# A scan and mixture-of-experts kernel: the output begins as x + D times the normalized row instead of as a copy of x

## The chip, the core and the metric

The kernel runs as one program on one core of a Trainium2 chip. The metric is the device time of one execution in microseconds (us); smaller is better. A core has TensorE (PE, matrix products; PEld is its weight load), VectorE (DVE), ScalarE (ACT), GpSimd (POOL) and SyncE (SP). [...] DMA transfers are issued from the queues of SP and POOL.

## The reference, cut to what matters

A layer normalization feeds two branches, and both are added to the input. The attention branch sorts the tokens of each batch into clusters, runs a selective state-space scan over the sorted sequence, and puts the result back in the tokens' own order. The other branch is a mixture of eight experts with two chosen for each token. x is 2 x 2048 x 256 floats.

```python
xn = _layernorm(x)                      # (x - mean) / sqrt(var + 1e-5)
...
def step(h, inp):                       # over the sorted tokens u = sorted xn
    dA = exp(d_t[..., None] * A)
    h = dA * h + (d_t * u_t)[..., None] * b_t[:, None, :]
    y = einsum('bdn,bn->bd', h, c_t)
...
return y + D[None, :, None] * u         # the term that the change moves
...
x = x + scan_branch(xn) + expert_branch(xn)
```

D is one number per channel (256 of them). The term D * u, put back into the tokens' order, is D * xn of the same token, so it does not depend on the sorting.

## The kernel before

**The front** (lines 134 to 1018) works on all 4096 tokens, eight tiles `xts[k]` of 128 partitions x 4 rows x 256 channels (and 4 columns for expert numbers and shares). VectorE finds mean and variance (L374, `find_norm` L405), TensorE finds scores of clusters and experts, ScalarE normalizes seven of the tiles in place (L429, 128x256 at a time) and VectorE the eighth (L433); each tile is then stored to the DRAM tensor `xn` (L437). `route` lists which tokens belong to which expert tile. Its function `list_tokens` runs eight rounds; each builds two bf16 factors `one` and `num` on VectorE (L327, L330, L337) and ScalarE (L336) and multiplies them on TensorE (L342). In the front these factors are taken from the pool `tok`, the eight buffers that the `xts` held. `sort_tokens` and `list_rows` make the same sort of list for the clusters. `small_weights` (L274) makes small constants, among them `diag`, the 128x128 matrices with D on the diagonal, one for each half of the channels.

**The output** is gathered by addition in DRAM. Each of its rows begins as the row of x: `begin_sums(k)` (L990) is a DMA of 512 KB from x to out, DRAM to DRAM, four of them early in the front and four at its end. Later the expert tiles and the scan pieces add their rows with indirect DMAs that accumulate (`add_rows`, L884, on POOL's queue). The first of these waits until all eight beginnings have landed.

**The scan** is cut into 8 pieces of 512 sorted tokens (two batches, four pieces each). A piece's rows are gathered (`gather_scan`, L628), turned into `u` (channels x tokens: TensorE L653, ScalarE copy L654), projected (L667, L674), copied to `xd` (L679) and sent through DRAM to be broadcast. From this come the step sizes `dl` and `du`. For the first piece that is `size_first` (L759), one chain through TensorE, ScalarE and VectorE; for the others `size` and `series` are spread over the piece before. A piece has 8 steps (4 quarters of the 16 states, 2 halves of the channels), a step 4 places. At each place VectorE multiplies (L840) and scans (L849) 128x512 elements, ScalarE makes the decay (L834), and TensorE turns the states of the step before (L861) and, at the last place, contracts them with the C rows (L870) into the PSUM tile `y` of that half.

That `y` is begun by `Piece.begin(h)` (L792): four matmuls `u` x `diag` per half, which put D * u there; the contractions then add to it, and ScalarE takes the sums out (L805). In the trace one float matmul has two records, so a piece has 16 records of line L796.

**The expert tiles**, 71 of 128 rows, are dealt among the places. A tile is three jobs: `up(0)` and `up(1)` (L954, 16 records each, the first with a tanh on ScalarE at L962), then `down` (L977, scaled out by ScalarE at L981 and added to the output). VectorE's two products, `silu` (L967) and `gate` (L971), follow their `up` two places later. The up products have one PSUM buffer each (`ps_h`, `bufs=1`), so the next tile's `up(0)` waits for `silu`, and `up(1)` for `gate`. The tiles' weights come by indirect DMA (L914) into three buffers. A planner with written-down costs (`at_place`, 0.9 for each `begin`) keeps the planned work on TensorE in a fixed ratio to that on VectorE, and so decides at which place a job goes. `keep_order` fixes each engine's order to that of the text.

**The lead** (L1078) stands between front and scan: the first seven jobs of the expert tiles, with the preparation of the first piece between them.

```python
lead = [
    [], [p.find_members], [], [lambda: p.turn(0), lambda: p.turn(1)],
    [lambda: p.project(0), lambda: p.project(1), p.end_projection, ..., p.size_first, ...],
    [], [lambda: p.begin(0), lambda: p.begin(1)],
]
```

Job 0 and 1 are `up(0)` and `up(1)` of expert tile 0, jobs 2 and 3 those of tile 1, job 4 is `down` of tile 0, jobs 5 and 6 are the up products of tile 2.

Of the kernel before, what the change touches and what calls it, by code (L numbers as in the profile page):

```python
# [39 lines left out]
F32 = mybir.dt.float32  # L40
BF16 = mybir.dt.bfloat16
I32 = mybir.dt.int32
AF = mybir.ActivationFunctionType
# [5 lines left out]
P = 128  # L49
# [7 lines left out]
def scan_moe_kernel(  # L57
# [47 lines left out]
    ps_h = ctx.enter_context(tc.tile_pool(name="ps_h", bufs=1, space=PSUM))  # L105
    ps_m = ctx.enter_context(tc.tile_pool(name="ps_m", bufs=2, space=PSUM))
    front = ctx.enter_context(ExitStack())
    tok = front.enter_context(tc.tile_pool(name="tok", bufs=8))
    sml = front.enter_context(tc.tile_pool(name="sml", bufs=1))
# [125 lines left out]
    nc.sync.dma_start(bias, dt_bias)  # L235
    dcol = cst.tile([P, ND], F32, name="dcol")
    nc.sync.dma_start(dcol, ds_)
    na = cst.tile([P, ND, NS], F32, name="na")
# [35 lines left out]
    def small_weights():  # L274

        diag = cst.tile([P, ND, P], F32, name="diag")
        for h in range(ND):
            nc.vector.tensor_scalar(diag[:, h, :], ident, dcol[:, h : h + 1], None, ALU.mult)


        cp = cst.tile([K, XP], F32, name="cp")
        nc.vector.memset(cp, 0.0)
        differ = cst.tile([P, ND, K], F32, name="differ")
        nc.vector.tensor_copy(differ[:, :, 0:1], chosen_by[:, :, 0:1])
        nc.vector.tensor_sub(differ[:, :, 1:], chosen_by[:, :, 1:K], chosen_by[:, :, 0 : K - 1])
        pc = ps_m.tile([K, NS], F32, tag="m", name="pc")
        for h in range(ND):
            nc.tensor.matmul(
                pc, lhsT=differ[:, h, :], rhs=pwT[:, h, :], start=h == 0, stop=h == ND - 1
            )  # L290
        nc.vector.tensor_copy(cp[:, R + NS :], pc)

        nc.scalar.activation(na, na, AF.Exp)
        nc.vector.tensor_scalar_mul(na, na, -1.0)
        return diag, cp

# [57 lines left out]
    def front_factors(width: int):  # L354

        one = tok.tile([P, P, LC], BF16, tag="tok", name="one")
        num = tok.tile([P, 3, width, LC], BF16, tag="tok", name="num")
        return one, num
# [46 lines left out]
    def find_norm():  # L405


        nm = sml.tile([P, BJ], F32, tag="nm", name="nm")
        nc.vector.tensor_add(nm, st[:, :, 1], st[:, :, 4])
# [11 lines left out]
        nc.vector.tensor_mul(nr, nm, rstd)  # L421
        return nm, rstd, nr

# [214 lines left out]
    class Piece:  # L638
# [152 lines left out]

        def begin(self, h: int):  # L792

            y = ps_s.tile([P, JC, P], F32, tag=f"y{h}", name=f"y{h}")
            for i in range(JC):
                nc.tensor.matmul(  # L796
                    y[:, i, :], lhsT=self.u[:, h, i * P : (i + 1) * P], rhs=diag[:, h, :],
                    start=i == 0, stop=False, skip_group_check=True,
                )
            self.ys[h] = y  # L800

        def take_sums(self, h: int):
# [21 lines left out]
    class Step:  # L824
# [19 lines left out]
        def scan(self, i: int):  # L844
            p, q, h = self.piece, self.q, self.h
            if i == 0:
                self.hs = late.tile([P, CH, Q], F32, tag="hs", name="hs", bufs=3)
            start = carry[:, q, h, i : i + 1] if p.c else 0.0
# [18 lines left out]
        def contract(self, i: int):  # L867
            p, q = self.piece, self.q
            for j in range(P // G):
                nc.tensor.matmul(  # L870
                    p.ys[self.h][j * G : (j + 1) * G, i, :],
                    lhsT=p.zs[q][:, i * (P // G) + j, :], rhs=self.ht[i][:, j, :],
                    start=False, stop=q == NQ - 1, skip_group_check=True,
                )
# [112 lines left out]
    n_x = len(xts)  # L987
    acc_rows = [(out_rows[r : r + CH, :], x.rearrange("b l d -> (b l) d")[r : r + CH, :]) for r in range(0, B * L, CH)]

    def begin_sums(k: int):  # L990
        nc.sync.dma_start(*acc_rows[k])

    for k in range(n_x):
# [4 lines left out]
        if k == n_x // 2:  # L998
            turn_scores(0)
        if k < n_x // 2:  # L1000
            begin_sums(k)
    score((n_x - 2, n_x - 1))
    turn_scores(1)
    nm, rstd, nr = find_norm()
    for k in range(n_x - 1):
# [8 lines left out]
    pieces[0].gather()  # L1014
    diag, cp = small_weights()
    for k in range(n_x // 2, n_x):
        begin_sums(k)
    front.close()
# [49 lines left out]
    for t in range(n_dealt + 1):  # L1068
        if t < n_dealt:
            jobs += [part_up(t, 0), part_up(t, 1)]  # L1070
        if t > 0:
# [3 lines left out]
    p = pieces[0]  # L1075


    lead = [  # L1078
        [], [p.find_members], [], [lambda: p.turn(0), lambda: p.turn(1)],
        [lambda: p.project(0), lambda: p.project(1), p.end_projection, lambda: p.load_b(0, Q), p.size_first,  # L1080
         *(lambda q=q: p.load_z(q) for q in range(NQ))],
        [], [lambda: p.begin(0), lambda: p.begin(1)],
    ]
    ahead = len(lead)
    for n, more in enumerate(lead):
# [4 lines left out]
        for _, do in later.pop(now, []):  # L1090
            do()
    for i in range(Q):
        steps[0].decay(i)
# [23 lines left out]
    for n, p in enumerate(pieces):  # L1117
# [3 lines left out]
        if n:  # L1121
# [16 lines left out]
            at_place(s1 + 5, NSUB - 1, lambda p=p: p.load_b(0))  # L1138
            at_place(s0, 3, lambda p=p: p.begin(0), 0.9)
            at_place(s0 + 1, 1, lambda p=p: p.begin(1), 0.9)  # L1140
        s2 = s0 + SP_
# [140 lines left out]
```

## Time and profile before

| what | value |
|---|---|
| three runs, median | 751.91 us (751.2 to 751.93) |
| the profiled execution | 752.28 us |
| its span, as in the profile | 750.5 us (1.8 us lie around it) |
| mean clock granted to TensorE | 0.951 of full speed |
| busy PE / PEld / DVE / ACT / POOL | 678.0 / 588.9 / 678.5 / 508.0 / 523.0 us |
| records of L796 (D * u on TensorE) | 128, mean 292 ns, 18.5 us in sum |
| DMAs x to out | 8 of 512 KB, 8.3 us to landing |

The span runs from the first instruction to the last. "Busy" counts an engine's time inside instructions; TensorE's records overlap each other (the pitch from one to the next is far below the mean duration), so its busy time is not the time that it needs. The chain is the work that ended last, followed back from release to release. A line with "idle before" tells how long an engine stood before an instruction and which engine released it.

### The profile page before, as it was taken

What the parts mean: (1) busy time and instruction counts of PE and PEld (TensorE: products, weight loads), DVE (VectorE), ACT (ScalarE), POOL (GpSimd) and SP (SyncE); (2) the same over time, 40 slices, a digit from 0 to 9 for tenths busy, and PEclk for the clock granted to TensorE, in tenths of its full rate; (3) what the DMA queues carried; (4) which work ended last, traced back from release to release, by engine and by line L of the source; (5) the groups of instructions that cost most, each with busy time, mean ns of one, the idle gap of its engine ahead of it and who ended that gap; (6) DMA issues with size and microseconds to landing.
All of it is one profiled execution on the core that took longest, in us unless ns stands there. A gap on an engine that the chain in (4) does not pass through costs nothing.

```text
span 750.5 us, 16877 instructions
## 1 busy us (share of the span) xinstructions
PE 678.0 (90%) x6506; PEld 588.9 (78%) x6506; DVE 678.5 (90%) x1085; ACT 508.0 (68%) x983; POOL 523.0 (70%) x362
## 2 busy tenths in 40 slices
PE   7375779999998999999999999999999998999993
PEld 5144678888877998888878898999798977899982
DVE  8885389899987999999999999999999997999991
ACT  4830446686758866886769577967795768767762
POOL 2023448667777788777877887788788888887733
PEclk9755979999999999999999999999999999999996
DMA  8676544584436755685458656865575547745312
GB/s 269 243 162 233 166 162 92 159 244 138 124 56 171 252 146 117 171 264 148 114 132 281 160 130 124 255 198 132 119 249 157 128 93 219 227 125 118 86 17 29
DMA packets 60401, 120.31 MB, mean 160 GB/s; under 512 B 24160, under 2 KB 41248, under 8 KB 53152
## 3 DMA queue, kind: packets, MB, share of 16 engines
q0 software_dynamic: 38784, 63.71, 36.0%
q1 hardware_dynamic: 21536, 55.50, 21.9%
q8 instruction: 52, 0.85, 0.5%
q14 instruction: 29, 0.24, 0.1%
HBM read 170.78 MB, written 22.28 MB: 257 GB/s over the span
## 4 chain that ended last, share of the span: by engine, by line
PE 69%; ACT 11%; DVE 9%; DMA 5%; issue 4%; POOL 1%; POOLq 0%; ACTq 0%; DVEq 0%
PE p_ps L954 29%; PE py L977 13%; PE pt_s L861 11%; PE y L870 7%; DMA w<-in_w_down_dram,w_row 3%; ACT ht L865 3%; PE y L796 2%; PE pl L342 2%; PE pt_g L937 2%; DMA out_dram<-yo,token_of 2%; ACT da L834 2%; DVE st L374 1%; ACT e L732 1%; ACT r L732 1%; PE px L667 1%
## 5 line engine op out<-in xcount | busy, mean ns | idle before, releaser
L954 PE MATMUL p_ps<-xT,w 128*128 128x128 f32 x2176 | 272.6, 281 | 12.3 <-DVE g L971 8.1
L954 PEld LDWEIGHTS p_ps<-xT,w 128*128 128x128 f32 x2176 | 258.0, 195 | 26.3 <-DVE g L971 8.3
L849 DVE TENSOR_TENSOR_SCAN hs<-da,carry,bu 128x512 f32<-128x512 f32 x192 | 246.0, 1281 | 0.0
L834 ACT ACTIVATE da<-dl,na 128x512 f32<-128x512 f32 x256 | 183.7, 734 | 0.2 <-DVE dl L789 0.2
L840 DVE TENSOR_TENSOR bu<-du,bt 128x512 f32<-128x512 f32 x256 | 173.1, 676 | 0.0
L865 ACT COPY ht<-pt_s 128x512 f32<-128x512 f32 x256 | 138.4, 595 | 40.3 <-PE pt_s L861 39.3
L895 POOL DMA_INDIRECT out_dram<-yo,token_of x68 | 131.4, 1932 | 48.0 <-ACT yo L981 22.6
L914 POOL DMA_INDIRECT w<-in_w_up_dram,w_row x68 | 91.8, 1350 | 89.2 <-DVE w_row L595 43.4
L861 PE MATMUL pt_s<-ident,hs 128*128 128x128 f32 x1024 | 136.8, 277 | 9.7 <-ACT ht L865 8.6
L977 PE MATMUL py<-w,g 128*128 128x256 f32 x544 | 129.8, 381 | 7.5 <-ACT xT L939 4.8
L861 PEld LDWEIGHTS pt_s<-ident,hs 128*128 128x128 f32 x1024 | 116.5, 142 | 21.4 <-ACT ht L865 13.4
L977 PEld LDWEIGHTS py<-w,g 128*128 128x128 f32 x544 | 98.0, 190 | 20.6 <-ACT xT L939 6.0
L928 POOL DMA_INDIRECT xg_sb<-xn,token_of x68 | 91.8, 1349 | 26.2 <-issue 12.8
L914 POOL DMA_INDIRECT w<-in_w_down_dram,w_row x68 | 94.7, 1392 | 20.7 <-issue 13.4
L895 POOL DMA_INDIRECT out_dram<-yt,line_of x32 | 66.1, 2065 | 23.0 <-issue 11.3
L849 DVE TENSOR_TENSOR_SCAN hs<-da,bu 128x512 f32<-128x512 f32 x64 | 78.1, 1221 | 0.0
L962 ACT ACTIVATE t_sb<-p_ps 128x512 f32<-128x512 f32 x68 | 41.0, 603 | 54.5 <-PE p_ps L954 54.4
L870 PE MATMUL y<-ht,z 128*32 128x128 f32 x2048 | 74.0, 277 | 1.5 <-PEq L1208 0.7
L981 ACT ACTIVATE yo<-py,own 128x256 f32<-128x256 f32 x68 | 32.3, 475 | 61.4 <-PE py L977 58.8
L967 DVE SCALAR_TENSOR_TENSOR t_sb<-t_sb,p_ps 128x512 f32<-128x512 f32 x68 | 45.8, 674 | 26.1 <-ACT t_sb L962 26.1
L870 PEld LDWEIGHTS y<-ht,z 128*32 128x32 f32 x2048 | 50.8, 109 | 19.6 <-issue 10.2
L632 POOL DMA_INDIRECT xs<-xn,line_of x32 | 41.8, 1306 | 14.7 <-issue 8.2
(202 smaller groups left out, 582.0 us busy)
## 6 DMA issues: line engine op xcount, KB each, us to landing
bt<-bc SPq DMA_DIRECT2D x31, 1024.0 KB, 5.1
z<-bc SPq DMA_DIRECT2D x32, 256.0 KB, 3.2
xn<-xt SPq DMA_DIRECT2D x8, 520.0 KB, 2.6
xt<-in_x_dram SPq DMA_DIRECT2D x8, 512.0 KB, 8.0
out_dram<-in_x_dram SPq DMA_DIRECT2D x8, 512.0 KB, 8.3
w<-in_w_up_dram,w_row POOLq DMA_INDIRECT x68
w<-in_w_down_dram,w_row POOLq DMA_INDIRECT x68
xg_sb<-xn,token_of POOLq DMA_INDIRECT x68
```

The source lines that it names most:

```text
L834: nc.scalar.activation(self.da[i], self.piece.dl[:, self.h, :], AF.Exp, scale=na[:, self.h, n : n + 1])
L840: nc.vector.tensor_mul(self.bu[i], self.piece.du[:, self.h, :], self.piece.bts[self.q][:, i, :])
L849: nc.vector.tensor_tensor_scan(self.hs[:, :, i], self.da[i], self.bu[i], start, ALU.mult, ALU.add)
L861: nc.tensor.transpose(pt[:, j, :], self.hs[:, t0 : t0 + G, :].rearrange("p t n -> p (t n)"), ident)
L865: nc.scalar.copy(self.ht[i], pt)
L870: nc.tensor.matmul(p.ys[self.h][j * G : (j + 1) * G, i, :], lhsT=p.zs[q][:, i * (P // G) + j, :], rhs=self.ht[i][:, j, :], start=False, st ...
L895: ins = nc.gpsimd.indirect_dma_start(out=out_rows, out_offset=bass.IndirectOffsetOnAxis(ap=numbers, axis=0), in_=rows, in_offset=None, com ...
L914: nc.gpsimd.indirect_dma_start(out=to[self.t % NW], out_offset=None, in_=rows, in_offset=bass.IndirectOffsetOnAxis(ap=w_row[:, self.t : se ...
L928: nc.gpsimd.indirect_dma_start(out=self.xg, out_offset=None, in_=xn_d, in_offset=bass.IndirectOffsetOnAxis(ap=token_of[:, self.t : self.t ...
L954: nc.tensor.matmul(p[:, f, :], lhsT=wk[:, h, f * P : (f + 1) * P], rhs=self.xT[:, h, :], start=h == 0, stop=h == ND - 1,)
L967: nc.vector.scalar_tensor_tensor(self.s, self.s, 1.0, self.p1, ALU.add, ALU.mult)
L977: nc.tensor.matmul(py, lhsT=self.g[:, f, :], rhs=w2[:, f, :], start=f == 0, stop=f == NH - 1)
```

## The change

The eight `xts` tiles live longer: their pool `tok` is moved to the other end of the memory and stays open through the lead. After a tile was normalized, it is turned into the row that the output begins with, in place. With std = (var + eps) * rstd and the row r already normalized,

(D + std) * r + mean = D * r + x.

VectorE does the first step (`scalar_tensor_tensor`, add then mult, 128x256), ScalarE adds the mean (Identity with the mean as bias, 128x256), four rows for each tile, so 32 instructions on each engine, and SP stores the tile to the output (8 DMAs of 512 KB from SBUF). This is spread over the first four jobs of the lead. The copies of x, `diag` and the 64 `u` x `diag` matmuls go, with the planner's 0.9 for each `begin`; the first contraction of a piece starts its PSUM tile. The factors `one` and `num` of the front are now in six buffers of the scan's `da` and four of `pre`'s `tok`. The states `hs` of the scan have a pool of their own, opened where the `xts` were, so the first scan waits until the eight stores are done.

```diff
+    rows_of = ctx.enter_context(ExitStack())
+    tok = rows_of.enter_context(tc.tile_pool(name="tok", bufs=8, side="right"))
-    tok = front.enter_context(tc.tile_pool(name="tok", bufs=8))
...
-    dcol = cst.tile([P, ND], F32, name="dcol")
-    nc.sync.dma_start(dcol, ds_)
+    drow = cst.tile([P, D], F32, name="drow")
+    nc.sync.dma_start(drow, ds_.partition_broadcast(P))
...
-        diag = cst.tile([P, ND, P], F32, name="diag")
-        for h in range(ND):
-            nc.vector.tensor_scalar(diag[:, h, :], ident, dcol[:, h : h + 1], None, ALU.mult)
...
-        one = tok.tile([P, P, LC], BF16, tag="tok", name="one")
-        num = tok.tile([P, 3, width, LC], BF16, tag="tok", name="num")
+        one = scn.tile([P, P, LC], BF16, tag="da", name="one", bufs=6)
+        num = pre.tile([P, 3, width, LC], BF16, tag="tok", name="num")
...
-        def begin(self, h: int):
-            y = ps_s.tile([P, JC, P], F32, tag=f"y{h}", name=f"y{h}")
-            for i in range(JC):
-                nc.tensor.matmul(
-                    y[:, i, :], lhsT=self.u[:, h, i * P : (i + 1) * P], rhs=diag[:, h, :],
-                    start=i == 0, stop=False, skip_group_check=True,
-                )
-            self.ys[h] = y
...
-                self.hs = late.tile([P, CH, Q], F32, tag="hs", name="hs", bufs=3)
+                self.hs = states.tile([P, CH, Q], F32, tag="hs", name="hs")
...
+            if q == 0 and i == 0:
+                p.ys[self.h] = ps_s.tile([P, JC, P], F32, tag=f"y{self.h}", name=f"y{self.h}")
...
-                    start=False, stop=q == NQ - 1, skip_group_check=True,
+                    start=q == 0 and i == 0, stop=q == NQ - 1, skip_group_check=True,
...
+    def find_rest():
+        nc.vector.tensor_mul(std, ve, rstd)
+        nc.vector.tensor_scalar_mul(mean, nm, -1.0)
     def begin_sums(k: int):
-        nc.sync.dma_start(*acc_rows[k])
+        for i in range(JC):
+            j = k * JC + i
+            row = xts[k][:, i, 0:D]
+            nc.vector.scalar_tensor_tensor(row, drow, std[:, j : j + 1], row, ALU.add, ALU.mult)
+            nc.scalar.activation(row, row, AF.Identity, bias=mean[:, j : j + 1])
+        b, j0 = k * JC // J, k * JC % J
+        nc.sync.dma_start(
+            out[b].rearrange("(p j) d -> p j d", j=J)[:, j0 : j0 + JC, :], xts[k][:, :, 0:D]
+        )
...
-        if k < n_x // 2:
-            begin_sums(k)
...
-    for k in range(n_x // 2, n_x):
-        begin_sums(k)
+    find_rest()
...
     lead = [
-        [], [p.find_members], [], [lambda: p.turn(0), lambda: p.turn(1)],
+        [p.find_members, begin(0), begin(1)], [begin(2), begin(3)], [begin(4), begin(5)],
+        [begin(6), lambda: p.turn(0), lambda: p.turn(1), begin(7)],
...
-        [], [lambda: p.begin(0), lambda: p.begin(1)],
+        [], [],
     ]
...
+    rows_of.close()
+    states = ctx.enter_context(tc.tile_pool(name="states", bufs=3, side="right"))
...
-            at_place(s0, 3, lambda p=p: p.begin(0), 0.9)
-            at_place(s0 + 1, 1, lambda p=p: p.begin(1), 0.9)
```

In the changed kernel `begin(k)` in the lead stands for `begin_sums(k)`; its three parts are lines L992 (VectorE), L993 (ScalarE) and L995 (the store).

More of the change, by code (lines that the diff above doesn't have):

```diff
@@ L294, in small_weights @@
         nc.vector.tensor_scalar_mul(na, na, -1.0)
-        return diag, cp
+        return cp
     def over(v, last_dim):
@@ L405, in find_norm @@
     def find_norm():
-        nm = sml.tile([P, BJ], F32, tag="nm", name="nm")
+        nm = cst.tile([P, BJ], F32, name="nm")
         nc.vector.tensor_add(nm, st[:, :, 1], st[:, :, 4])
@@ L421, in find_norm @@
         nc.vector.tensor_mul(nr, nm, rstd)
-        return nm, rstd, nr
+        return nm, rstd, nr, ve
     def normalize(k: int, on_act: bool):
@@ L987, in scan_moe_kernel @@
     n_x = len(xts)
-    acc_rows = [(out_rows[r : r + CH, :], x.rearrange("b l d -> (b l) d")[r : r + CH, :]) for r in range(0, B * L, CH)]
-    def begin_sums(k: int):
-        nc.sync.dma_start(*acc_rows[k])
+    std = cst.tile([P, BJ], F32, name="std")
+    mean = cst.tile([P, BJ], F32, name="mean")
+    def find_rest():
+        nc.vector.tensor_mul(std, ve, rstd)
+        nc.vector.tensor_scalar_mul(mean, nm, -1.0)
+    def begin_sums(k: int):
+        for i in range(JC):
[7 more added lines that the diff above has]
+        )
     for k in range(n_x):
@@ L999, in scan_moe_kernel @@
             turn_scores(0)
-        if k < n_x // 2:
-            begin_sums(k)
     score((n_x - 2, n_x - 1))
     turn_scores(1)
-    nm, rstd, nr = find_norm()
+    nm, rstd, nr, ve = find_norm()
     for k in range(n_x - 1):
@@ L1014, in scan_moe_kernel @@
     pieces[0].gather()
-    diag, cp = small_weights()
-    for k in range(n_x // 2, n_x):
-        begin_sums(k)
+    cp = small_weights()
+    find_rest()
     front.close()
@@ L1075, in scan_moe_kernel, with begin @@
     p = pieces[0]
+    def begin(k: int):
+        return lambda: begin_sums(k)
     lead = [
-        [], [p.find_members], [], [lambda: p.turn(0), lambda: p.turn(1)],
+        [p.find_members, begin(0), begin(1)], [begin(2), begin(3)], [begin(4), begin(5)],
+        [begin(6), lambda: p.turn(0), lambda: p.turn(1), begin(7)],
         [lambda: p.project(0), lambda: p.project(1), p.end_projection, lambda: p.load_b(0, Q), p.size_first,
          *(lambda q=q: p.load_z(q) for q in range(NQ))],
-        [], [lambda: p.begin(0), lambda: p.begin(1)],
+        [], [],
     ]
@@ L1265 @@
         "a_logs": columns(L0_attn_A_logs),
-        "ds": columns(L0_attn_Ds),
+        "ds": np.asarray(L0_attn_Ds)[None],
         "w_up": np.concatenate([rows(L0_ffn_w1), rows(L0_ffn_w3)], axis=2),
```

## The prediction

> **What bounds the kernel now.** I read the page's shares and its chain first, then the waits of the scan stage (98 to 740 us), then the ScalarE and TensorE rows of the lead.
>
> ```profile
> PE 678.0 (90%) x6506; PEld 588.9 (78%) x6506; DVE 678.5 (90%) x1085; ACT 508.0 (68%) x983; POOL 523.0 (70%) x362
> ...
> PE 69%; ACT 11%; DVE 9%; DMA 5%; issue 4%; POOL 1%; POOLq 0%; ACTq 0%; DVEq 0%
> PE p_ps L954 29%; PE py L977 13%; PE pt_s L861 11%; PE y L870 7%; DMA w<-in_w_down_dram,w_row 3%; ACT ht L865 3%; PE y L796 2%; PE pl L342 2%; PE pt_g L937 2%; DMA out_dram<-yo,token_of 2%; ACT da L834 2%; DVE st L374 1%; ACT e L732 1%; ACT r L732 1%; PE px L667 1%
> ```
>
> TensorE and VectorE are equally busy, but the chain runs through TensorE, and L796 is 2% of it. The waits of the scan stage (us in total, times, longest) tell who waits for whom:
>
> ```profile
> DVE t_sb L967 <- ACT t_sb L962: 20.2, 12, 4.4
> ...
> PE pt_s L861 <- ACT ht L865: 8.6, 17, 2.2
> ...
> PE p_ps L954 <- DVE g L971: 8.1, 1, 8.1
> ...
> PE py L977 <- ACT xT L939: 4.8, 5, 1.4
> ...
> DVE one L327 <- PE pl L342: 2.3, 1, 2.3
> ```
>
> VectorE waits 20.2 us for a tanh, which itself waits for TensorE's up products; with the list's waits it stands some 24 us between 98 and 735 us. TensorE waits for VectorE once, at the end of the lead (8.1 us), and else only for ScalarE's copies. So in the scan TensorE is late and VectorE meets it at a few places: a gain there is at most those 24 us. In six windows of 20 us from 420 to 540, and again from 640 to 720, VectorE hardly stands at all (19.8 to 20.0 busy of 20).
>
> **1. What goes from TensorE in the scan.** Sixteen L796 records per piece. At full clock sixteen records of the same shape (p_ps, L954) take 1.79 us in the chain, so seven pieces give 7 x 1.79 = 12.5 us. The first piece's stand at low clock:
>
> ```profile
> 98.19 3.78 PE p_ps L954 x16
> 101.97 2.77 PE y L796 x16
> ```
>
> That is 2.8 us more; 15.3 in sum. VectorE's steady work is unchanged, so I take the gain from its idle places, in a piece at most about what TensorE loses there (its rows with "idle before" in the timeline; idle, then what I take): 109-110 us, straight behind the first L796: 2.1, take 2.1. 133-136, the list of the second batch: 3.3, of which the same round trip costs 1.9 in the front, where nothing else is queued (0.93 + 0.99); take 0.7 of the rest. 149-197: 1.0, take 0.5. 224 and 241: 7.7, take 1.8. 318: 1.3, take 0.9. 395: 2.1, take 1.3. 546: 0.8, take 0.6. 594-636: 5.6, take 1.6. Sum **-9.5 us**. Bounds: TensorE alone limits, all 15.3; VectorE limits, nothing; below nothing, a loss of about 3, since with 0.9 less at each begin the planner deals jobs up to three places off their old ones, and one wait of the largest sort (4.4 at 241) could come anew. I stay at 9.5 because no TensorE wait for VectorE stands against it.
>
> [...]
>
> **2. The front.** The list's factors no longer share the buffers of `xts`. VectorE's rows show what the sharing cost:
>
> ```profile
> 37.87 0.68 DVE L327 TENSOR_TENSOR one<-idx_p,f 128x1024 bf16<-128x1024 bf16 x1
> 40.83 0.46 DVE L330 TENSOR_TENSOR num<-idx_p,f 128x568 bf16<-128x568 bf16 x1 [2.27 <-PE pl L342]
> ```
>
> The second `num` waits until the first round's matmuls release a buffer; in the changed instruction list it waits for nothing. The chain runs along VectorE from here to 51, where TensorE takes the last four rounds (8.41 us); its earlier rounds are then done by about 47.5, before it is wanted at 48.9. So -2.3 us, and -0.4 for the two `diag` instructions (0.39 in the chain): **-2.7**, bounds 0 (another late buffer) and -2.7. The eight copies of x that go are waited for by nothing there: 0. `find_rest`, two small VectorE operations (0.2 us each, row L294), lies behind `cp` while TensorE turns: 0.
>
> **3. The lead.** Now 32 operations on each of VectorE and ScalarE are issued among the first four jobs.
>
> VectorE: `scalar_tensor_tensor` of 128x512 takes 0.61 from start to start (chain, L784); 256 elements less, at the 515 ns between its 512 (683) and 1024 (1198) forms, give 0.35. The first sixteen run from 71.5 to 77.1, so `silu` of tile 0, at 75.84 now, ends at 77.8 instead of 76.5; `up(0)` of tile 1 is wanted at 77.7, and so is `gate`: no delay. The other sixteen end by 84, where VectorE stands till 89.63 anyway. Cost 0; with 0.43 each (row L433, 406 ns, and a gap) 1.3 us, hidden behind ScalarE.
>
> ScalarE is where it is paid:
>
> ```profile
> 75.21 0.60 ACT L962 ACTIVATE t_sb<-p_ps 128x512 f32<-128x512 f32 x1 [3.45 <-PE p_ps L954]
> 79.53 0.60 ACT L962 ACTIVATE t_sb<-p_ps 128x512 f32<-128x512 f32 x1 [3.72 <-PE p_ps L954]
> 81.75 1.07 ACT L654 COPY u<-pt_u 128x512 f32<-128x512 f32 x2 [1.63 <-PE pt_u L653]
> 82.92 0.37 ACT L939 COPY xT<-pt_g 128x256 f32<-128x256 f32 x1
> 84.91 0.47 ACT L981 ACTIVATE yo<-py,own 128x256 f32<-128x256 f32 x1 [1.62 <-PE py L977]
> 86.51 0.37 ACT L679 COPY xd<-px 128x256 f32<-128x256 f32 x1 [1.13 <-PE px L674]
> ```
>
> Its idle time here (3.45) lies before the first tanh, and the order by engine puts all the new operations behind that. Identity with a bias column at 128x512 (L739) takes 723 ns; 256 elements less at 0.853 ns (L782 622 ns at 512, L743 1059 at 1024) give 505, and starts follow 0.1 closer than durations (L834: 734 long, 3.17 for five, so 0.61 to 0.63 apart): 0.41 us. Bounds 0.36 (L732 from PSUM, start to start) and 0.49 (L429, two columns). From 75.7: sixteen to 82.3, the second tanh to 82.8, twelve to 87.7; then come the `u` copies, which stand at 81.75 now. **+5.9** (4.5 to 8.2). Four more lie behind the copies and delay only `xT` and `yo`, hidden by py and px. Behind `u` wait TensorE's px, then `xd`, pd, e, w, dl, du and the first scan, one chain up to 98 us, with nothing to absorb it.
>
> Second, TensorE now stands from 82.1 to 88.2 before pt_g, py and px. What standing costs is seen at 98.19: after 8.1 us idle sixteen records took 3.78, not 1.79, the next sixteen 2.77, together 3.0 more. At 236 us a gap of 2.16 cost about 1.6 (p_ps 3.21), while one as long at 631 left pt_s at its usual 1.14. For 6.1 us: **+2.0**, bounds 0 and 3.0. [...]
>
> The stores: 8 x 512 KB from 77 to about 91, each of the kind `xn<-xt` (520 KB, 2.6 us to landing; 8.0 for the loads of x, all at once). The last lands by 99 at the latest; the first adding DMA (POOL, 85.66 now) waits for them, and behind it POOL stands 13.6 us till 102.25 today; the first scan, with the shared buffer, is due at 105. On SP the `bc` stores come behind them, due at 92. Cost 0. If traffic made a store land 7 us later than that, the scan would wait 1 us.
>
> **Sum**, against the profiled execution (752.28: span 750.5 and 1.8 around it): -2.7 + 5.9 + 2.0 - 9.5 = -4.3, so 748.0. The median of three, 751.91, lies 0.37 lower, so **747.6**. About 0.2%, 1.5 us, is what a measurement can tell from no change.
>
> **The cases.**
> A, 0.46: the sum above, own range 744 to 750.3.
> B, slower, 0.26: VectorE limits the scan, and TensorE's freed time becomes TensorE idle. Place: pieces 1 to 7; the front and the lead stand, +5.2, and only the 2.1 behind the first L796 and about 1 more come back. 752.28 + 5.2 - 3 = 754.5, less 0.37: 754.1. It decides as soon as the gain in the scan is under 3.7. For it: the windows without VectorE idle. Against: TensorE waits for VectorE nowhere in the scan.
> C, 0.12: TensorE's lead is carried from piece to piece and all 15.3 come back: 742.2, say 742. For it: the chain's 2%. Against: TensorE's own waits for ScalarE (20 us) do not shrink.
> D, 0.16: the lead is at its upper bounds (8.2 + 3.0 instead of 7.9) and the rest as in A: 751, no change that can be told. For it: the row L429 and the 3.0 at 98 us.
> That the D * u term does not really go is excluded: the changed instruction list has 64 matmuls less.
>
> Chances: faster A + C = 0.58, same D = 0.16, slower B = 0.26. The range 742 to 756 leaves out about half of C, and of B the part with a loss in the scan.
>
> **What would show it.** Right: `num` without idle before it near 38.6; the `u` copies at about 85 (87.7 less 2.7) behind a row of L993; a first scan near 105 instead of 99.86; VectorE's waits for t_sb down from 20 to about 12. Wrong: a first scan before 102 or after 108; L993 outside 0.36 to 0.49; waits for t_sb still near 20, or new TensorE waits for VectorE (B); a first scan that waits for the stores.

## The result, and the profile after

The changed kernel takes **755.76 us** (median of 5, 753.76 to 758.22), the kernel before 751.93 (5 runs, 751.2 to 752.58): a ratio of 1.0055 [1.0039, 1.0071]. It is slower by about 4 us where I forecast 4 less. On another chip, with ten runs, the ratio was 1.0052 [1.0029, 1.0076]. The profiled execution was the fastest of the five, 753.76; that of before lay 0.35 above its median. Every ratio here is taken from fast runs alone (a run more than 1.5% above the fastest of its kernel is left out), while the medians further down are those of all runs.

Three numbers divide the span. They are read from the rows of the first up product (L944, was L954) and of the scans (L837, was L849):

| us | before | after | change | forecast |
|---|---|---|---|---|
| start of the first up product (end of the front) | 71.39 | 69.23 | -2.2 | -2.7 |
| from there to the first scan (the lead) | 28.47 | 35.32 | +6.9 | +7.9 |
| from the first scan to the last (the scan) | 634.1 | 631.5 | -2.6 | -9.5 |

"Scan" is counted from the start of the first scan instruction to the start of the last. Front and lead came nearly as forecast: the first scan starts at 104.55 (I wrote "near 105"). What lies behind the last scan is 0.7 us shorter. Seven of the nine and a half microseconds that the scan should have won are missing. First the page's shares and its chain, after:

```profile
PE 668.5 (89%) x6378; PEld 574.8 (76%) x6378; DVE 691.3 (92%) x1117; ACT 519.3 (69%) x1015; POOL 533.7 (71%) x362
...
PE 69%; ACT 15%; DVE 6%; DMA 4%; issue 3%; POOL 1%; POOLq 0%; SPq 0%; ACTq 0%; DVEq 0%
```

PE has 128 records and 9.5 us less, its share of the chain stays 69%, and ACT's rises from 11 to 15%. The waits of the scan stage say where TensorE's time went (us in total, times, longest):

```profile
DVE t_sb L957 <- ACT t_sb L952: 17.3, 10, 3.1
...
PE pt_s L849 <- ACT ht L853: 9.7, 21, 2.2
...
PE p_ps L944 <- DVE g L961: 9.1, 2, 8.1
...
PE pt_u L651 <- DMA xs<-xn,line_of: 4.0, 2, 3.8
```

VectorE still waits 17.3 us for the tanh (20.2 before; I forecast about 12), and the last row is new: TensorE waits for the gathered rows of a piece. A second wait of TensorE for VectorE is new too, 1.0 us at 582.

Front and lead line by line. VectorE's second `num` no longer stands before it starts (before: 2.27):

```profile
37.56 0.45 DVE L328 TENSOR_TENSOR num<-idx_p,f 128x568 bf16<-128x568 bf16 x1
39.08 0.45 DVE L328 TENSOR_TENSOR num<-idx_p,f 128x568 bf16<-128x568 bf16 x1
```

and ScalarE's queue ahead of the `u` copies (start, duration, then the instruction; the part in brackets is the idle time before it and who ended it):

```profile
72.69 0.60 ACT L952 ACTIVATE t_sb<-p_ps 128x512 f32<-128x512 f32 x1 [3.08 <-PE p_ps L944]
73.19 6.48 ACT L993 ACTIVATE xt<-xt,mean 128x256 f32<-128x256 f32 x16
79.57 0.58 ACT L952 ACTIVATE t_sb<-p_ps 128x512 f32<-128x512 f32 x1
80.05 4.89 ACT L993 ACTIVATE xt<-xt,mean 128x256 f32<-128x256 f32 x12
84.84 1.05 ACT L652 COPY u<-pt_u 128x512 f32<-128x512 f32 x2
```

Sixteen additions of the mean in 6.48 are 0.405 each (forecast 0.41), and `u` comes at 84.84 (forecast "about 85"). Behind `u` TensorE's `py` takes 3.58 us instead of 1.99, at a granted clock of 0.55 in the mean of these 3.58 us instead of 1.00 (before, then after):

```profile
82.88 1.99 PE L977 MATMUL py<-w,g 128*128 128x256 f32 x8
85.94 3.58 PE L967 MATMUL py<-w,g 128*128 128x256 f32 x8
```

Two things in the lead I had not foreseen. POOL's second gather for the first piece took 0.95 us before; now POOL's timeline has:

```profile
69.70 7.14 POOL L630 DMA_INDIRECT xs<-xn,line_of  x1 [0.30 <-DVE member L657]
...
77.14 0.94 POOL L630 DMA_INDIRECT xs<-xn,line_of  x1 [0.30 <-issue]
```

VectorE's timeline at the same time:

```profile
69.61 6.40 DVE L992 SCALAR_TENSOR_TENSOR xt<-drow,std,xt 128x256 f32<-128x256 f32 x16
```

The gather ends at 76.84, 0.83 us behind the run of sixteen. A second run of sixteen (77.33 to 83.75) has three of POOL's transfers within it, at 1.00 to 1.22 us each; a fourth, begun at 82.55, takes 2.04 and ends behind the run.

The other is TensorE's. `up(0)` of tile 1 waits for `silu`, which now stands on VectorE behind the first run (75.94; the forecast had "no delay"):

```profile
76.67 3.84 PE L944 MATMUL p_ps<-xT,w 128*128 128x128 f32 x32 [2.23 <-DVE t_sb L957]
```

Both are hidden here, since ScalarE has no idle time between the tanh at 72.69 and `u`.

And the place in the scan. TensorE's timeline at the turning of the fifth piece:

```profile
364.41 0.38 PE L651 MATMUL pt_u<-ident,xs 128*128 128x128 f32 x2
364.94 0.33 PE L651 MATMUL pt_u<-ident,xs 128*128 128x128 f32 x1 [0.15 <-DMA xs<-xn,line_of]
369.11 0.48 PE L651 MATMUL pt_u<-ident,xs 128*128 128x128 f32 x1 [3.83 <-DMA xs<-xn,line_of]
369.51 1.94 PE L860 MATMUL y<-ht,z 128*32 128x128 f32 x32
```

VectorE's rows with idle time behind it:

```profile
374.38 0.69 DVE L961 SCALAR_TENSOR_TENSOR g<-t_sb,p_ps 128x512 f32<-128x512 f32 x1 [0.63 <-PE p_ps L944]
381.23 0.69 DVE L957 SCALAR_TENSOR_TENSOR t_sb<-t_sb,p_ps 128x512 f32<-128x512 f32 x1 [2.57 <-ACT t_sb L952]
395.94 0.69 DVE L957 SCALAR_TENSOR_TENSOR t_sb<-t_sb,p_ps 128x512 f32<-128x512 f32 x1 [2.42 <-ACT t_sb L952]
```

TensorE comes to the turning 1.0 us after POOL began to issue the last of its four gathers. In the trace of before there were 12 us between the two (POOL after; POOL and TensorE before):

```profile
363.39 0.95 POOL L630 DMA_INDIRECT xs<-xn,line_of  x1 [0.30 <-DMA xs<-xn,line_of]
...
356.49 2.06 POOL L632 DMA_INDIRECT xs<-xn,line_of  x1 [0.30 <-issue]
...
368.49 0.60 PE L653 MATMUL pt_u<-ident,xs 128*128 128x128 f32 x4
```

Of the 11 us that went, 4.1 are TensorE's coming earlier and 6.9 POOL's issuing later: the new dealing moved POOL's work too. TensorE stands 3.83 us, the contraction behind it takes 1.94 instead of 1.08, and VectorE stands 5.6 us at three places (2.05 at one of them before).

**VectorE's idle time accounts for the scan.** I added up VectorE's waits of 0.35 us and more between the first scan and 740 us, and took the sum from the scan's length: 634.1 - 23.1 = 611.0 before, 631.5 - 20.4 = 611.1 after, and 610.5 to 612.6 in all eighteen profiles of this study. The scan is 611 us of VectorE's work (with its gaps under 0.35 us), whatever TensorE has to do, and its idle time. So the change could win at most 23, and the question is place by place what became of the 23.

### The profile page after: what moved, and what is told of

Its sections match the earlier page's. It is cut to its first block, busy times and chain, and to the rows that moved or that the text cites. A ratio compares the mean times of both kernels' runs of the same rounds, so it can differ in the third digit from the quotient of the medians.

```text
span 751.9 us, 16690 instructions
## 1 busy us (share of the span) xinstructions
PE 668.5 (89%) x6378; PEld 574.8 (76%) x6378; DVE 691.3 (92%) x1117; ACT 519.3 (69%) x1015; POOL 533.7 (71%) x362
## 4 chain that ended last, share of the span: by engine, by line
PE 69%; ACT 15%; DVE 6%; DMA 4%; issue 3%; POOL 1%; POOLq 0%; SPq 0%; ACTq 0%; DVEq 0%
PE p_ps L944 29%; PE py L967 14%; PE pt_s L849 11%; PE y L860 6%; ACT ht L853 4%; ACT da L822 3%; DMA w<-in_w_down_dram,w_row 2%; PE pt_g L927 2%; PE pl L340 1%; DMA xs<-xn,line_of 1%; ACT xt L993 1%; PE pt_x L380 1%; PE pd L712 1%; ACT e L730 1%; ACT r L730 1%
## 5 line engine op out<-in xcount | busy, mean ns | idle before, releaser
L944 PE MATMUL p_ps<-xT,w 128*128 128x128 f32 x2176 | 272.8, 281 | 14.3 <-DVE g L961 9.1
L944 PEld LDWEIGHTS p_ps<-xT,w 128*128 128x128 f32 x2176 | 257.4, 195 | 29.8 <-DVE g L961 9.6
L837 DVE TENSOR_TENSOR_SCAN hs<-da,carry,bu 128x512 f32<-128x512 f32 x192 | 245.7, 1280 | 0.0
L885 POOL DMA_INDIRECT out_dram<-yo,token_of x68 | 133.2, 1958 | 58.9 <-issue 19.3
L849 PE MATMUL pt_s<-ident,hs 128*128 128x128 f32 x1024 | 135.9, 276 | 10.6 <-ACT ht L853 9.7
L904 POOL DMA_INDIRECT w<-in_w_up_dram,w_row x68 | 88.9, 1307 | 68.0 <-DVE w_row L593 41.6
L849 PEld LDWEIGHTS pt_s<-ident,hs 128*128 128x128 f32 x1024 | 115.0, 141 | 24.1 <-ACT ht L853 16.1
L904 POOL DMA_INDIRECT w<-in_w_down_dram,w_row x68 | 97.6, 1436 | 20.7 <-issue 14.9
L885 POOL DMA_INDIRECT out_dram<-yt,line_of x32 | 70.1, 2192 | 23.5 <-issue 8.5
L860 PE MATMUL y<-ht,z 128*32 128x128 f32 x2048 | 75.8, 279 | 5.5 <-ACT ht L853 4.0
L837 DVE TENSOR_TENSOR_SCAN hs<-da,bu 128x512 f32<-128x512 f32 x64 | 78.1, 1220 | 0.0
L957 DVE SCALAR_TENSOR_TENSOR t_sb<-t_sb,p_ps 128x512 f32<-128x512 f32 x68 | 45.7, 673 | 17.3 <-ACT t_sb L952 17.3
L630 POOL DMA_INDIRECT xs<-xn,line_of x32 | 47.7, 1490 | 15.2 <-issue 7.9
```

What stands on the lines that cost most here:

```text
L630: nc.gpsimd.indirect_dma_start(out=xs[:, i, :], out_offset=None, in_=xn_d, in_offset=bass.IndirectOffsetOnAxis(ap=line_of[b][:, q : q + 1] ...
L837: nc.vector.tensor_tensor_scan(self.hs[:, :, i], self.da[i], self.bu[i], start, ALU.mult, ALU.add)
L849: nc.tensor.transpose(pt[:, j, :], self.hs[:, t0 : t0 + G, :].rearrange("p t n -> p (t n)"), ident)
L860: nc.tensor.matmul(p.ys[self.h][j * G : (j + 1) * G, i, :], lhsT=p.zs[q][:, i * (P // G) + j, :], rhs=self.ht[i][:, j, :], start=q == 0 an ...
L885: ins = nc.gpsimd.indirect_dma_start(out=out_rows, out_offset=bass.IndirectOffsetOnAxis(ap=numbers, axis=0), in_=rows, in_offset=None, com ...
L904: nc.gpsimd.indirect_dma_start(out=to[self.t % NW], out_offset=None, in_=rows, in_offset=bass.IndirectOffsetOnAxis(ap=w_row[:, self.t : se ...
```

## The experiments

My theory after the result: front and lead are priced nearly right, and in the scan the planner's new dealing of the jobs (the 0.9 per `begin` is gone) gave back what the missing matmuls won (R), above all where it brings TensorE to a piece's turning before the gather has landed (G). The rival is B of the forecast: VectorE limits the scan, and TensorE's freed time was never worth more.

The chips differ: on two of them (15 and 10) the kernel before takes 765 us, on the others (the first, 9 and 6) 752. So every ratio is to the kernel before on the same chip.

| kernel | chip | median us | before there | ratio |
|---|---|---|---|---|
| e1_no_du | 15 | 763.68 | 765.72 | 0.9993 [0.9968, 1.0018] |
| e2_no_du_old_deal | 15 | 753.38 | 765.72 | 0.9839 [0.9812, 0.9865] |
| e3_after_old_deal | 15 | 755.22 | 765.72 | 0.9893 [0.9853, 0.9933] |
| a2_after_again | 15 | 765.99 | 765.72 | 0.9987 [0.9960, 1.0013] |
| f5_gather_early | 10 | 761.15 | 764.55 | 0.9963 [0.9934, 0.9993] |
| f4_no_mean | 10 | 761.17 | 764.55 | 0.9958 [0.9924, 0.9992] |
| f2_lead_spread | 10 | 756.09 | 764.55 | 0.9889 [0.9843, 0.9935] |
| e3_again | 9 | 751.56 | 751.96 | 1.0008 [0.9976, 1.0039] |
| f6_lead_spread2 | 9 | 747.36 | 751.96 | 0.9938 [0.9924, 0.9951] |
| f7_size_split | 9 | 748.52 | 751.96 | 0.9967 [0.9948, 0.9986] |
| f8_spread_and_split | 9 | 746.13 | 751.96 | 0.9924 [0.9909, 0.9938] |
| a3_after | 6 | 755.40 | 751.96 | 1.0052 [1.0029, 1.0076] |
| f5_again | 6 | 752.12 | 751.96 | 1.0009 [0.9983, 1.0035] |
| d1_before_redealt | 6 | 759.24 | 751.96 | 1.0098 [1.0081, 1.0115] |
| d2_front_only | 6 | 750.35 | 751.96 | 0.9983 [0.9973, 0.9992] |

### The D * u matmuls alone, dealt anew and as before

`e1_no_du` is the kernel before without `begin`, `diag` and the planner's 0.9, the first contraction starting the PSUM tile; `e2_no_du_old_deal` keeps the 0.9:

```diff
-            at_place(s0, 3, lambda p=p: p.begin(0), 0.9)
-            at_place(s0 + 1, 1, lambda p=p: p.begin(1), 0.9)
+            at_place(s0, 3, lambda: None, 0.9)          # e2 alone
+            at_place(s0 + 1, 1, lambda: None, 0.9)      # e2 alone
```

> The kernel before, without D * u: the begin matmuls, diag and the planner's 0.9 for each begin go, the first contraction starts its PSUM tile; x is copied to the output as before, nothing is done in the lead (the output lacks D times the normalized row). It measures the gain in the scan by itself. Theory 1 (the scan gives back little, since the waits that go are replaced by others; the changed kernel's VectorE waits sum to 20.4 us against 23.9): 747 to 750, a gain of 2 to 5. Rival (the scan gives back the forecast 9.5, and something else in the changed kernel eats it): 741 to 744. If VectorE limits wholly: 750 to 751.

> As the run without D * u, but the planner still counts 0.9 for each begin, so every job of the expert tiles stays at its old place. If the re-dealt jobs bring new waits, this is faster than the run without D * u, by 3 to 6 us (741 to 745). If the dealing does not matter, the two agree within 1.5 us.

(Both leave D * u out of the output.) The same matmuls are gone in both, and 10 us lie between them, more than the 3 to 6 that I expected: idle time in the scan 27.5 us in e1, 18.4 in e2. In e1's profile TensorE stands 3.4 us for `xs` at 449, and VectorE 3.04 and 3.90 behind it; another 2.3 of the 9 are a longer wait at 135 for which the trace names no releaser. The absolute times that I expected were for a chip of the first one's speed.

### The whole change, with the old dealing and as it is

`e3_after_old_deal` is the changed kernel with the two lines of e2 put in; `a2_after_again` is the changed kernel itself.

> The changed kernel with the planner's 0.9 for each begin kept, nothing else. If re-dealing costs the gain: 750 to 752. If not: 755 to 757, as the changed kernel itself.

> The changed kernel once more, for a second profile and for the spread: its five runs lay between 753.8 and 758.2, those before between 751.2 and 752.6. If the late gather of the first piece (the second of its DMAs took 7.14 us on POOL) or the slow landing of bc (6.1 us before the bt loads) varies from run to run, the first scan starts at another time than 104.55 in this profile; if the spread comes from the scan, it starts within 0.3 us of it and the waits for t_sb differ.

Again 10 us: a scan of 631.4 us and 20.0 idle with the old dealing, 643.7 and 31.6 with the new, where TensorE stands 4.0 us for `xs` at 379. The first scan is at 105.1 and 104.9, so the 10 us are not the lead's; against the first profile's 104.55 this is 0.35 us, a little over the 0.3 asked, so the changed kernel's spread is in the main the scan's. This shows that the loss is the dealing's, but on a chip on which the kernel before was 14 us slower.

### Once more on a chip of the first one's speed

> The changed kernel with the old dealing (the planner's 0.9 per begin kept) once more, beside the next three kernels on their chip. All theories: first scan at 105.1 within 0.5 us, a scan stage of 611.5 us plus VectorE's idle time in it, and a ratio to the kernel before near the 0.989 of its first run; theory R (the re-dealing of the jobs, not the chip, made the changed kernel slower than this one) has it under 0.994, the rival (it was that chip) lets it rise to 1.0.

The ratio is 1.0008: by the limits that I set the rival won, and the 0.989 belonged to a chip on which the kernel before loses 14 us. What is left of R is smaller: beside the 1.0052 and 1.0055 of the changed kernel at this speed the old dealing is 3 to 4 us better, from different chips and with intervals that touch. The profiled execution (749.84) has a scan of 627.6 us, 6.5 less than before, and 16.9 idle. Six of its ten runs took 748.9 to 752.5, four 756.7 to 763.5; what the four lost, no profile shows.

### The gather alone

```diff
-            at_place(max(s1 - 1, 0), 1 if n > 1 else 0, p.gather)
+            at_place(max(s1 - (2 if n > 1 else 1), 0), 1 if n > 1 else 0, p.gather)
```

> The changed kernel with each gather of the next piece's rows (from the third piece on) put one step, four places, earlier; nothing else. Theory G (what the scan gained was given back because TensorE, dealt less work ahead of a piece's turning, comes to it before the gather has landed; 3.8 us of waiting at 369 us in the changed kernel's trace, then records at half rate and 3.2 us of VectorE waits): the waits of pt_u for xs are gone, the lateness against the kernel before stays near -8 us after piece 3, and the time is 4 to 6 us under that of the changed kernel. Rival B (VectorE and the big waits for t_sb at 240 and 637 us set the scan; the gather's wait would only have been another wait): no change beyond 1.5 us.

On chip 10, without the changed kernel beside it, it was 0.9963; a2 on chip 15 had been 0.9987, and the intervals overlap. Its profile has no wait for `xs` and yet 27.2 us idle, against 20.0 with the old dealing on chip 15 (0.9893): on the slower chips the late gather is not all that the new dealing costs. So the pair was run on one chip:

> The changed kernel, unchanged, as the mark for the next run. All theories: first scan at 104.5 to 104.9, scan stage 611 us plus VectorE's idle time there. If this chip times the kernel before near 752 us, 754 to 758 us; if near 765, about the same as the kernel before.

> The changed kernel with the next piece's gather one step earlier, beside the changed kernel on one chip. Theory G (the late gather is the place where the re-dealing costs): 3.5 to 5.5 us under the changed kernel, no TensorE wait for xs near 369 us, VectorE's idle time in the scan down from some 20 to 15 us. Rival (the jobs' new places cost of themselves, wherever a ScalarE burst meets them): less than 1.5 us under it, the idle time coming back at other places.

3.3 us less (752.12 against 755.40), just under the 3.5 to 5.5 that G forecast and far from the rival's 1.5; the intervals, 1.0009 [0.9983, 1.0035] and 1.0052 [1.0029, 1.0076], overlap by a little. In a3 the late gather fell on the next piece, TensorE's rows:

```profile
446.54 0.48 PE L651 MATMUL pt_u<-ident,xs 128*128 128x128 f32 x1 [4.84 <-DMA xs<-xn,line_of]
446.81 3.62 PE L944 MATMUL p_ps<-xT,w 128*128 128x128 f32 x16
```

and VectorE's two waits behind it:

```profile
450.46 0.69 DVE L961 SCALAR_TENSOR_TENSOR g<-t_sb,p_ps 128x512 f32<-128x512 f32 x1 [4.62 <-PE p_ps L944]
458.97 0.69 DVE L957 SCALAR_TENSOR_TENSOR t_sb<-t_sb,p_ps 128x512 f32<-128x512 f32 x1 [2.04 <-ACT t_sb L952]
```

The up product behind the stand took 3.62 instead of some 1.95. Until there a3 had been 9.3 us ahead of the kernel before, counted from the first scan; eight scans later it was 2.5. f5_again has no such wait and passes the same scans at 9.6 ahead. Its idle time is 16.4, a3's 25.0. From 537 us on it gives back 2.9, at waits for a tanh. So G holds at this speed: with the gather early, the new dealing costs nothing against the old one (16.4 us idle here, 16.9 in e3_again on chip 9). The new dealing is not needed for such a wait: f2, with the old one, stands 2.47 us for `xs` at 528.

### The new dealing in the kernel before

The two `at_place` lines of `begin` without their 0.9, D * u still on TensorE.

> The kernel before, D * u kept on TensorE, with the planner's 0.9 for each begin taken away, so that the jobs are dealt as in the changed kernel. Theory R (the new dealing is the loss): 3 to 6 us slower than the kernel before on the same chip, with VectorE's idle time in the scan up by as much, or more, since the D * u products now come unplanned. Rival: dealing does not matter here, within 1 us of the kernel before.

759.24, 7.3 us slower, more than R's 3 to 6; its profiled run (761.85, the slowest of four) has a scan 5.5 us longer than the first profile, with 27.5 us idle, none of it behind a gather, and a front 3.3 us longer (first up product at 74.66) for which no run shows a reason. The dealing costs here too, by other places. That it does so because the planner no longer knows of the D * u products is my reading; no run separates it from the mere move of the jobs.

### The second profile of before

> The kernel before, unchanged, for a second profile of it beside those of the next three kernels. Theory S (the scan of one and the same kernel differs between executions by when a gather or a weight lands, while front and lead do not): first scan at 99.9 within 0.5 us, and a scan stage from first to last scan that may differ from the first profile's 634 us by several us. Rival: the scan stage is fixed by the order of instructions; then both are within 1 us of the first profile.

On chip 10: the first scan at 101.3 instead of 99.9 within 0.5, so the lead is not as fixed as S had it; the scan 645.0 us, 33.3 of it idle. Of the 10 us more than in the first profile, 3.0 are one wait at 137 for which the trace names no releaser, 2.2 a longer wait for a tanh at 402, the rest small ones. The scan of one kernel does differ by idle time alone, as S says; whether from execution to execution or from chip to chip this pair does not tell.

### What the lead's price is

`f4_no_mean` is the changed kernel without L993; `f2_lead_spread` has the old dealing and this lead, in which `begin(k, False)` adds the mean on VectorE:

```diff
-        [p.find_members, begin(0), begin(1)], [begin(2), begin(3)], [begin(4), begin(5)],
-        [begin(6), lambda: p.turn(0), lambda: p.turn(1), begin(7)],
-        [lambda: p.project(0), ...
+        [p.find_members, begin(0), begin(1)], [begin(3, False)], [begin(2), begin(5)],
+        [lambda: p.turn(0), lambda: p.turn(1), begin(6), begin(4, False)],
+        [begin(7), lambda: p.project(0), ...
```

> The changed kernel without the 32 additions of the mean on ScalarE (L993); the rows stored lack the mean. Theory Q (the lead's price is ScalarE's queue, and the cold TensorE behind it): the u copies come back from 84.8 to about 79 to 80 us, TensorE stands for less than 3 us before them, and the first scan comes at 97 to 99 us instead of 104.55. Rival M (the lead's price is memory traffic and the gathers held up on POOL by the run of scalar_tensor_tensor on VectorE): first scan at 102 or later. In both, if POOL's second gather of the first piece again takes some 7 us instead of 1, the VectorE run holds it, not ScalarE's work.

> The changed kernel with the old dealing (the planner's 0.9 per begin kept) and another lead: behind job 0 two tiles of rows, behind job 1 one whose mean VectorE adds, behind job 2 two, then the turning of the first piece, one tile as before and one with VectorE's addition, and the last one behind them; 24 instead of 32 additions on ScalarE, 20 of them before the u copies instead of 28. From the row L993 (0.405 us each): 8 x 0.405 = 3.2 us less before the u copies, and TensorE stands about 3 us less, 1 us of clock: first scan at 100 to 101 us instead of 105, and the time about 4 us under that of the kernel with the old dealing alone, which on its chip was 0.989 of the kernel before; so 0.982 to 0.986. If the scan absorbs the lead's gain (rival: its big waits depend on weights that land at a fixed time), the ratio stays at 0.989.

f4: the lead is 31.2 us long instead of 35.3, the first scan at 100.2. The 35.3 are of another chip, though. On f4's own chip the changed lead took 33.5 (f5_gather_early, where `py` ran in 1.99 us) and that of the kernel before 29.8 (b2). So of a price of 3.7 us there, 2.3 go with ScalarE's additions and 1.4 stay. What stays are the two things from the result, now in the open: TensorE stands for `silu`, and 1.15 us for the gather, which again took 7.14:

```profile
76.39 3.84 PE L944 MATMUL p_ps<-xT,w 128*128 128x128 f32 x32 [2.23 <-DVE t_sb L957]
...
81.70 0.76 PE L651 MATMUL pt_u<-ident,xs 128*128 128x128 f32 x5 [1.15 <-DMA xs<-xn,line_of]
```

I had expected 97 to 99; between the two theories it is Q with a part of M, and both of TensorE's waits come with VectorE's run.

f2: the forecast of 100 to 101 failed, 107.0. VectorE's row ahead of the first scan says why:

```profile
105.71 1.34 DVE L828 TENSOR_TENSOR bu<-du,bt 128x512 f32<-128x512 f32 x2 [5.28 <-DMA bt<-bc]
```

My last store stood behind job 4, whose adding DMA writes to the same output, so SP waited 12.5 us for it, and the `bc` stores behind it on SP came at 99.46 instead of 91.56. The ratio, 0.9889, is the rival's, but what the trace shows in the way is this wait, and not weights. Its POOL row also answers to the 7.14:

```profile
69.14 4.37 POOL L630 DMA_INDIRECT xs<-xn,line_of  x1 [0.30 <-DVE member L657]
```

and VectorE's rows beside it:

```profile
69.05 3.63 DVE L992 SCALAR_TENSOR_TENSOR xt<-drow,std,xt 128x256 f32<-128x256 f32 x9
72.72 0.35 DVE L996 TENSOR_SCALAR xt<-xt,mean 128x256 f32<-128x256 f32 x1
72.99 0.48 DVE L992 SCALAR_TENSOR_TENSOR xt<-drow,std,xt 128x256 f32<-128x256 f32 x1
73.50 0.35 DVE L996 TENSOR_SCALAR xt<-xt,mean 128x256 f32<-128x256 f32 x1
```

Nine in a row, to 72.68, then additions of the mean between: the gather ends at 73.51, again 0.83 us behind the run. Without L992 (e1, e2) it takes 1.10.

`f6_lead_spread2` takes the last tile forward, `begin(7, False)` behind `begin(4, False)`:

> The old dealing and the spread lead again, but the last tile of rows is finished (mean on VectorE) and stored ahead of the first down job, so that no store waits for an adding DMA. In the first form of this lead the bc stores stood on SP behind such a store until 99.46, and the first multiplication waited 5.28 us for bt. Theory Q (ScalarE's queue and the clock behind it are the lead's price): first scan at 101 to 102 us without a wait for bt, 3 to 4 us under the kernel with the old lead of the same chip. Rival (the 4 MB of stores are the price, since bc lands only behind them): a wait for bt of 2 us or more remains and the first scan is at 104 or later.

First scan at 102.02, no wait for `bt`, 2.3 us earlier than e3_again, as Q has it; the median is 4.2 lower, the profiled execution 1.2 (748.67 and 749.84), so how much of the 4.2 is the lead and how much e3_again's four long runs is open.

### The two large waits

```diff
             self.step_size(0)
-            self.step_size(1)
+            half_sizes.append(lambda: self.step_size(1))
...
+            while half_sizes:                              # at the next place
+                half_sizes.pop(0)()
```

`f7_size_split` has this with the old dealing, `f8_spread_and_split` with the old dealing and the lead of f6.

> The old dealing, and the eight ScalarE instructions that make a piece's step sizes given out in two groups of four, the second one place later, behind the turning's copies. Theory Z (VectorE's waits of 4.4 us at 246 and 4.6 at 638 are ScalarE's: eight in a row, 2.9 us, ahead of the ht copies, so TensorE stands 2.15 us, then runs its next up product at a lower clock, 3.2 instead of 2.05 us): ScalarE's half of the burst and the slow product go, 1.45 + 1.2 us, and each of the two waits falls to about 1.7; 5 us in sum against the kernel with the old dealing. Rival L (TensorE's load in that piece is the cause, so relief on TensorE alone moves these waits): they stay at 4 or more.

> The two last edits together: spread lead and split step sizes, on the old dealing. If both terms are independent, 3.4 us in the lead and 5 in the scan: 8 us under the kernel with the old dealing, a ratio of 0.977 to 0.981 to the kernel before. If the waits that go come back elsewhere, no better than the better of the two.

TensorE's timeline around 238 us with the old dealing (e3_again):

```profile
238.22 1.35 PE L849 MATMUL pt_s<-ident,hs 128*128 128x128 f32 x8 [2.16 <-ACT ht L853]
239.36 3.42 PE L944 MATMUL p_ps<-xT,w 128*128 128x128 f32 x16
```

and the same place in f7:

```profile
236.97 1.15 PE L850 MATMUL pt_s<-ident,hs 128*128 128x128 f32 x8 [0.70 <-ACT ht L854]
237.95 1.95 PE L945 MATMUL p_ps<-xT,w 128*128 128x128 f32 x16
```

Both terms of Z are there: 1.46 less standing, 1.47 less on the product. VectorE's wait in the kernel before, in e3_again and in f7:

```profile
241.47 0.69 DVE L967 SCALAR_TENSOR_TENSOR t_sb<-t_sb,p_ps 128x512 f32<-128x512 f32 x1 [4.43 <-ACT t_sb L962]
243.45 0.69 DVE L957 SCALAR_TENSOR_TENSOR t_sb<-t_sb,p_ps 128x512 f32<-128x512 f32 x1 [4.44 <-ACT t_sb L952]
242.85 0.69 DVE L958 SCALAR_TENSOR_TENSOR t_sb<-t_sb,p_ps 128x512 f32<-128x512 f32 x1 [3.62 <-ACT t_sb L953]
```

It fell only from 4.44 to 3.62 (forecast 1.7), and the one at 633 from 4.58 to 3.81; VectorE's idle time is 14.9 instead of 16.9, 1.9 less and not 5. In f7 the tanh starts at 242.24, 2.3 us after its product, and ScalarE has no idle time ahead of it from 234.87 on. So what is left of the wait is ScalarE's own queue, more of it than Z had. Relief on TensorE alone does not move it (4.43 and 4.44), and the rival L falls. Under the new dealing, where other jobs meet there, it is 1.86. f8 takes both edits: 746.13, a ratio of 0.9924; 5.4 us under the median of the kernel with the old dealing (5.7 by the profiled executions) instead of the 8 forecast, and the fastest of those that compute the whole output.

### The front alone

```diff
-        one = tok.tile([P, P, LC], BF16, tag="tok", name="one")
-        num = tok.tile([P, 3, width, LC], BF16, tag="tok", name="num")
+        one = scn.tile([P, P, LC], BF16, tag="da", name="one", bufs=6)
+        num = pre.tile([P, 3, width, LC], BF16, tag="tok", name="num")
```

> The kernel before with the list's two factors in the scan's and the preparation's buffers and nothing else changed. By the forecast's first term the second num waits for nothing, the last score product of the front ends 1.7 to 2.3 us earlier, and so do the first up product and the first scan (97.6 to 98.2 instead of 99.86); since the scan stands at its own places, 1.7 to 2.3 us less in the whole. Rival: the wait comes back at the last rounds, where TensorE is the limit, and the first scan moves by less than 0.8 us.

Against the first profile of before, the first up product starts 1.64 earlier (69.75), the first scan 2.7 (97.2), and the median is 1.6 lower than before's on its chip, near the 1.7 to 2.3 expected. The front's term holds; the scan of its profile gave 1.2 back.

## Why the prediction was wrong

**The front: right**, -2.2 for -2.7; the second `num` waits for nothing.

**The lead: right in size, and in part in its reason.** +5.9 for ScalarE's queue and +2.0 for the clock were forecast, 6.9 came: `u` starts 15.6 us after the first up product instead of 10.4 (+5.2), and the way from `u` to the first scan is 1.6 longer, as `py` is. The queue's 0.405 each is as worked out. That the clock's term came is in part chance: in f5_gather_early, with the same lead, `py` took 1.99 us, and behind equal stands of 1.68 us it took 3.04 in f6 and 2.00 in f8. Two limits lie under ScalarE's queue, `silu` and the gather behind VectorE's run; f4 shows them, 1.4 us on its chip. I had costed L992 at 0.35 us each (it takes 0.40) and by VectorE's own queue alone, with "no delay" for the products.

**The scan: wrong, -9.5 forecast, -2.6 measured.** Two terms failed: the gain added up by places, 9.5, is 6.2 where the dealing is kept, and the re-dealing, which I set at nothing, costs 3.5 of these (idle time 23.1 before, 16.9 with the old dealing, 20.4 after; profiles of two chips of like speed). VectorE's waits by place, all of 0.35 us and more:

| about, us | before | forecast gain | left, old dealing (e3_again) | left, after |
|---|---|---|---|---|
| 109 to 112 | 2.13 | 2.1 | 0 | 0 |
| 133 to 140, the list | 3.30 | 0.7 | 2.54 | 2.44 |
| 149 to 205 | 0.37 | 0.5 | 2.20 | 1.45 |
| 224 to 247 | 7.69 | 1.8 | 6.65 | 1.86 |
| 311 to 325 | 1.32 | 0.9 | 0 | 1.85 |
| 374 to 397 | 2.05 | 1.3 | 0 | 5.62 |
| 445 to 475 | 0 | 0 | 0 | 0.38 |
| 536 to 580 | 0.84 | 0.6 | 0 | 3.63 |
| 604 to 680 | 5.43 | 1.6 | 5.48 | 3.13 |
| sum | 23.1 | 9.5 | 16.9 | 20.4 |

With the old dealing 6.2 of the 9.5 come. The small waits, where TensorE was just late, go altogether, more than I took. The large ones at 241 and 633 do not shrink, since it is ScalarE's queue that makes them. A new one of 1.8 stands at 152. I had asked only what TensorE loses at each place; the stand of 2.16 us at 236 that I quoted for the clock ended on `ht`, a ScalarE copy, and could have told me who is late there.

Then the dealing. I named it as a loss of about 3 and set it at nothing "because no TensorE wait for VectorE stands against it". That looked at the wrong partner: the wait that came is for a DMA. The dealing itself takes 4.8 us out at 224 to 247 and puts 11.5 in at 311 to 580 us, half of it behind the one gather. f5_again takes the gather away, and the sum is 16.4.

**Median against profile**: I took 0.37 off; the profiled run of after lay 2.0 under its median. The late gather falls on the piece at 369 in one execution and on that at 446 in another, which fits the changed kernel's spread of 4.5 us over five runs, where the kernel before has 1.4.

**Rival B** gave the time that came nearest of the four cases: 754.1 for a median of 755.76, 754.5 for the profiled 753.76. Its mechanism is half of it: VectorE's 611 us are fixed, and only its idle time can be won. But it let only 3 us come back, and 6.2 do when the dealing is kept; that the time fits so well is luck, since the other half, what the re-dealing costs, was in the bounds and not in its story.

Left open: what the four long runs of e3_again lost; what ends VectorE's waits of 3.4 to 5.3 us at 133 to 138 us in five profiles on the chips that were slower, where the trace names no releaser; what the new dealing costs on the slower chips besides the gather; and the old and the new dealing side by side on one chip of the first one's speed, which were not run.

## What to carry to other kernels

Where one engine's work in a stage is the same before and after, take its busy work from the stage's length and look at what is left: a change elsewhere can win only that rest, and each wait in it has to be followed to the engine that is late, not to the one named last. A cost written into a planner is part of the kernel: taking it out with the work it stood for moves everything behind it, so change the work and the dealing in two steps. When an engine gets faster, check how long before its use each transfer is issued: here 12 us had shrunk to 1, the larger part because POOL issued it later.

## What the runs showed of the hardware

- **One of POOL's gathers took long beside a run of L992 on VectorE.** With sixteen in a row (6.40 us) this indirect DMA took 7.14 us instead of 0.95; with nine (3.63, f2) it took 4.37; without them (e1, e2) 1.10. Both long ones ended 0.83 us behind the run. Not every transfer was long: three ran in 1.00 to 1.22 us within the second run of sixteen. Which are, and why, no run here shows.
- **A slow product came behind a stand of 2.16 us**: 3.42 us (e3_again, with a granted clock of 0.50 between 239.0 and 242.4 us; in the kernel before, at the same stand, 3.42 with 0.51 between 237.0 and 240.4). Behind a stand of 0.70 it took 1.95 (f7). The length of the stand alone did not decide it: behind the stand of 2.16 at 631 in the kernel before the clock was 1.00 and the product took 1.95, and equal stands of 1.68 gave 3.04 and 2.00 us for `py` (f6 and f8).
- **What came behind the stores on SP landed later.** With 4 MB of rows under way (350 GB/s in the mean between 79 and 93 us, 132 in the kernel before) the 32 KB `bc` stores of the first piece took 6.9 us to land instead of 1.7, and `bt` could be issued 7.3 us after `bc` instead of 2.9. The first scan did not wait for it.
